# A graph network of four layers on one core: a third of every other attention unit's masking goes from VectorE to GpSimd

## The chip, the core and the metric

The kernel runs on one core of a Trainium2 chip. The core has five engines that run their own instruction streams and wait for one another by semaphores: TensorE (PE in the profile; its weight loads are listed apart as PEld), VectorE (DVE), ScalarE (ACT), GpSimd (POOL) and SyncE (SP), which here only issues DMAs. The metric is the device time of one execution in microseconds (us); lower is better.

## The reference

The input is x with 3327 nodes of 512 features, and a sparse adjacency matrix adj of 3327 x 3327, whose density falls with the node numbers. Four layers follow one another, each as x = x + layer(relu(layernorm(x)), adj). Layers 0, 2 and 3 are graph attentions with 8 heads of 64 features; layer 1 (SAGE) takes the mean of the neighbours and three products with 512 x 512 matrices. An attention, in short:

```python
Wh = h @ W                                  # per head: n x 64
e = leaky_relu(s_dst[i] + s_src[j])         # per head, for each pair (i, j)
e = where(adj[i, j] > 0, e, NEG)
out[i] = softmax_j(e) @ Wh                  # per head
```

Layer 0 then normalises its columns over the nodes and applies a relu; layers 2 and 3 apply an elu.

## The kernel before, in words

The nodes are padded to 26 blocks of 128. The work on a target side is done in 52 groups of 64 targets. Since adj is sparse, each group has a list of the sources that it needs, in chunks of 128 sources; the number of chunks is fixed per group (the table CAPS, from 22 for the first group to 5 and 4 for the last), 359 chunks in all. The lists are made in the first part of the kernel.

The softmax is taken apart so that no exponential is needed for a pair: exp(leaky_relu(a + b)) is the larger of two products of one factor of the target and one of the source. With a common factor taken out, one max per pair and head is left: the weight of source j for target i is max(r[i], v[j]) times the mask. The row sum comes from a 65th column of the features.

The function attend does one attention. A unit is 2 or 3 chunks of one group, 135 units per layer (89 of 3 chunks, 46 of 2). Per unit:

- load (L1240) gathers the source rows. The helper gather (L1164, L1165) issues one indirect DMA on the GpSimd queue per chunk: 128 rows of a table in DRAM, named by the list idx. A row holds the features and the factors v of all heads. The tile rows has 6 buffers. In layer 0 a row also holds the words of the adjacency; there load unpacks them on DVE (on, L1252) and ACT (mask, L1258) into the SBUF tile mask, which layers 1, 2 and 3 read again.
- DVE takes the max (mx, L1266) of r_bc, the group's target factors spread over all partitions in PSUM by a small matmul (L1198), and of the source factors in rows. The tile mx lies in PSUM and has one buffer.
- DVE multiplies mx with the mask (wgt, L1273) into SBUF, 3 buffers. The free size is 8 heads x 64 targets = 512 elements per chunk, so 1536 or 1024 per instruction.
- PE accumulates (facc, L1287): per chunk and head, wgt is the stationary operand and 65 columns of rows the moving one; the profile shows 16 matmul records per chunk.
- When a group ends, ACT copies the sums (L1215), DVE takes reciprocals (L1219), ACT scales (L1225), and for every second group finish adds the residual and stores.

The function later advances these endings by one step per unit, and with them, in layer 2, the projection of the next layer's features (tick), and in layer 0 small independent matmuls (beside).

Inside attend the order of instructions on PE, DVE and ACT is that of the program (manual_schedule). Pool is not in that list, so the planner orders its instructions; in attend Pool has nothing but the gathers. In the program load(i + 1) stands behind unit i's mult, and how far Pool runs ahead of the other engines is limited only by the 6 row buffers.

Of the kernel before, what the change touches and what calls it, by code (L numbers as in the profile page):

```python
# [23 lines left out]
F32 = mybir.dt.float32  # L24
# [3 lines left out]
I32 = mybir.dt.int32  # L28
# [4 lines left out]
ALU = mybir.AluOpType  # L33
ET = mybir.EngineType
# [4 lines left out]
P = 128  # L39
H = 8  # L40
F = 64
# [9 lines left out]
GB = 64  # L51
# [4 lines left out]
LNB = 5  # L56
ROW = H * (F + 1) + H
UNIT = 3
SUNIT = 2
SROWS = 8  # L60
SAHEAD = 2
# [1075 lines left out]
def sparse(ctx: ExitStack, tc: tile.TileContext, t: dict, out: bass.AP, WA, ls, cs, idx, rdeg, first):  # L1137
# [5 lines left out]
    nc = tc.nc  # L1143
# [18 lines left out]
    mask = keep.tile([P, NCH, GB], U8, name="mask")  # L1162

    def gather(dst, src, k):  # L1164
        nc.gpsimd.indirect_dma_start(  # L1165
            out=dst, out_offset=None, in_=src[:, :], in_offset=bass.IndirectOffsetOnAxis(ap=idx[:, k : k + 1], axis=0)
        )


    def attend(layer, table, r_dram, finish, tick=lambda: None, home=None):  # L1170

        width = table.shape[1]
        units = []
        for g in range(ls.G):
            mine = list(ls.batches(g, UNIT))
            units += [(g, k0, n, i == 0, i == len(mine) - 1) for i, (k0, n) in enumerate(mine)]
        hq = H // PG  # L1180
        sw = hq * (F + 1)
        with tc.tile_pool(name=f"fatt{layer}", bufs=2) as ap, tc.tile_pool(
            name=f"facc_ps{layer}", bufs=2, space=PSUM
        ) as aps, tc.manual_schedule(engines={ET.PE, ET.DVE, ET.Activation}):
            rows, rrs, rbs, accs, ends = {}, {}, {}, {}, []

            def fetch(g):
                if g < ls.G:
                    rr = ap.tile([2, H * GB], F32, name="r_two", tag="r_two", bufs=3)
                    nc.sync.dma_start(rr, r_dram[g, :, :, :].rearrange("t h i -> t (h i)"))  # L1190
                    rrs[g] = rr

            def spread(g):


                if g < ls.G:
                    rb = aps.tile([P, H * GB], F32, name="r_bc", tag="r_bc", bufs=2)
                    nc.tensor.matmul(rb, ones[0:2, :].bitcast(F32R), rrs.pop(g).bitcast(F32R), start=True, stop=True)  # L1198
                    rbs[g] = rb.rearrange("p (h i) -> p h i", i=GB)

            def ending(g, hps={}):

                b, u = divmod(g, PG)
                if u == 0:
                    hps[b] = home[:, b, :] if home is not None else None
                    if home is None:
                        hp_ = ap.tile([P, D], F32, name="fhp", tag="hp", bufs=3)
                        hps[b] = hp_
                hp, o0 = hps[b], u * GB
                fin = finish(b, hp, ap)  # L1210
                if u == PG - 1:
                    next(fin)
                yield
                sm = ap.tile([P, sw], F32, name="sums", tag="sums", bufs=4)
                nc.scalar.copy(sm, accs.pop(g)[:, :sw])  # L1215
                sm = sm.rearrange("p (q x) -> p q x", x=F + 1)
                yield
                rd = ap.tile([P, hq, 1], F32, name="rd", tag="rd", bufs=4)
                nc.vector.reciprocal(rd, sm[:, :, F : F + 1])  # L1219
                yield  # L1220
                for v in range(PG):
                    mine = slice(v * GB, (v + 1) * GB)
                    for q in range(hq):
                        h = q * PG + v
                        nc.scalar.mul(hp[o0 : o0 + GB, h * F : (h + 1) * F], sm[mine, q, 0:F], rd[mine, q, :])  # L1225
                yield
                if u == PG - 1:
                    del hps[b]
                    yield from fin

            def later():
                for e in list(ends):
                    if next(e, 0) == 0:
                        ends.remove(e)
                tick()

            for g in range(2):
                fetch(g)
            spread(0)
            def load(i):  # L1240

                if i >= len(units):
                    return
                g, k0, n, _, _ = units[i]
                gi = ap.tile([P, UNIT, width], I32, name="rows", tag="rows", bufs=6)
                rows[i] = gi.bitcast(F32)
                for k in range(n):
                    gather(gi[:, k, :], table, k0 + k)
                if layer == 0:
                    nw = GB // WB  # L1250
                    on = ap.tile([P, UNIT, nw, WB], U16, name="on", tag="on")
                    nc.vector.tensor_tensor(  # L1252
                        on[:, :n],
                        gi[:, :n, ROW:].bitcast(U16)[:, :, g * nw : (g + 1) * nw].unsqueeze(3).to_broadcast([P, n, nw, WB]),
                        cs["bit"].unsqueeze(1).unsqueeze(1).to_broadcast([P, n, nw, WB]),
                        ALU.bitwise_and,
                    )
                    nc.scalar.activation(mask[:, k0 : k0 + n, :], on[:, :n].rearrange("p k w b -> p k (w b)"), AF.Sign)  # L1258

            load(0)  # L1260
            for i, (g, k0, n, begins, stops) in enumerate(units):
                gt = rows.pop(i)
                mk = mask[:, k0 : k0 + n, :]
                full = [P, n, H, GB]
                mx = aps.tile([P, UNIT, H, GB], F32, name="mx", tag="mx", bufs=1)
                nc.vector.tensor_tensor(  # L1266
                    mx[:, :n],
                    rbs[g].unsqueeze(1).to_broadcast(full),
                    gt[:, :n, H * (F + 1) : ROW].unsqueeze(3).to_broadcast(full),
                    ALU.max,  # L1270
                )
                wt = ap.tile([P, UNIT, H, GB], F32, name="wgt", tag="wgt", bufs=3)
                nc.vector.tensor_tensor(wt[:, :n], mx[:, :n], mk.unsqueeze(2).to_broadcast(full), ALU.mult)  # L1273
                load(i + 1)
                later()
                if begins:
                    fetch(g + 2)
                    acc = aps.tile([P, BANK], F32, name="facc", tag="acc")
                    accs[g] = acc
                    spread(g + 1)  # L1280

                for k in range(n):
                    f, l = begins and k == 0, stops and k == n - 1
                    for q in range(hq):
                        for v in range(PG):
                            h = q * PG + v
                            nc.tensor.matmul(  # L1287
                                accs[g][v * GB : (v + 1) * GB, q * (F + 1) : (q + 1) * (F + 1)],
                                wt[:, k, h, :],
                                gt[:, k, h * (F + 1) : (h + 1) * (F + 1)],  # L1290
                                start=(f and q == 0),
                                stop=(l and q == hq - 1),
                            )
                if stops:
                    ends.append(ending(g))
            while ends:
                later()
# [32 lines left out]
    with ExitStack() as mx:  # L1330
# [48 lines left out]
        with tc.tile_pool(name="beside", bufs=1) as wp, tc.tile_pool(name="beside_ps", bufs=1, space=PSUM) as wps:  # L1379
            bg = beside(wp, wps)  # L1380

            def done(c, hp, pool):
                yield
                whole.append(c)
                yield

            attend(0, *first, done, lambda: next(bg, None), y)
            for _ in bg:
                pass
# [91 lines left out]
        def tick():  # L1481
            for e in list(ends):
                if next(e, 0) == 0:
                    ends.remove(e)
            proj.tick()
# [3 lines left out]
        for b in range(NB):  # L1489
            ps = list(zip_longest(*(list(ls.batches(b * PG + u, SUNIT)) for u in range(PG))))  # L1490
            parts += [(b, p, i == 0, i == len(ps) - 1) for i, p in enumerate(ps)]
        loaded = {}

        def load(i):
# [3 lines left out]
            for u, kn in enumerate(parts[i][1]):  # L1498
                if kn is not None:
                    k0, n = kn  # L1500
                    zt = gp.tile([P, SUNIT, D], F32, name="z_rows", tag="z_rows", bufs=SROWS)
                    mf = gp.tile([P, SUNIT, GB], F32, name="z_mask", tag="z_mask", bufs=SROWS)
                    nc.scalar.copy(mf[:, :n, :], mask[:, k0 : k0 + n, :])  # L1503
# [7 lines left out]
        for i, (b, _, begins, stops) in enumerate(parts):  # L1511
# [4 lines left out]
            for r, u, k, m, z in loaded.pop(i):  # L1516
# [3 lines left out]
                g = b * PG + u  # L1520
# [102 lines left out]
```

## Time and profile before

| | |
|---|---|
| median of 3 runs | 2915.1 us (2900.37 to 2917.88) |
| profiled execution | 2553.76 us, its span 2551.8 us |
| mean granted TensorE clock in it | 0.851 of full speed |
| mx L1266, wgt L1273 (DVE) | 405 instructions each, 639.4 and 638.4 us |
| rows L1165 (Pool gathers of the attentions) | 1077 instructions, 1027.7 us |
| facc L1287 (PE) | 17232 matmuls, 722.5 us |

One execution was profiled. Busy time is the time in which an engine runs an instruction; the idle time in front of a group of instructions is put down to what ended it. "issue" means that the engine waited for nothing that the profile shows. In the order of time: lists and the projection of layer 0 until 319 us, attention 0 until about 806 us, column statistics and layer 1 until about 1430 us, attention 2 until about 2010 us with layer 3's projection beside it, attention 3 from 2046 us to the end.

### The profile page before, as it was taken

To read this page: it belongs to the slowest core of one execution; us is meant where nothing else is said; L and a number is where in the kernel's file an instruction comes from. 1 tells how busy PE (TensorE), PEld (TensorE's weight loads), DVE (VectorE), ACT (ScalarE), POOL (GpSimd) and SP (SyncE) were. 2 spreads that over 40 slices of the span, in tenths; PEclk is the share of its full clock that TensorE was granted. 3 is DMA by queue.
4 is the path that set the end of the run, shared out by engine and by line. 5 is a ranking of instruction groups with operands and counts; after the bars stand their busy time and mean duration, and the time that the engine had idled before them with its cause. 6 is when DMAs were issued, how large, how long until landed. Compare 5 with 4: busy or idle time off the path is not lost.

```text
span 2551.8 us, 53690 instructions
## 1 busy us (share of the span) xinstructions
PE 1825.0 (72%) x21112; PEld 1161.8 (46%) x21112; DVE 1852.3 (73%) x2272; ACT 1068.3 (42%) x3810; POOL 1387.4 (54%) x1482
## 2 busy tenths in 40 slices
PE   3667756776677698889999657778878646566653
PEld 2444444454454342223333356656555435555543
DVE  7667579999997850222333499999877279999996
ACT  4553212333445332334455214667766601233444
POOL 1000176777772026777777277776554067777672
PEclk9767889988888899999999778897877787777787
DMA  8773198888783566788888478887665178888784
GB/s 326 288 263 123 43 296 276 280 281 260 241 253 95 191 217 198 234 247 260 254 267 255 125 223 242 235 240 232 199 200 177 39 215 232 236 238 243 232 238 123
DMA packets 189057, 562.57 MB, mean 220 GB/s; under 512 B 37764, under 2 KB 42304, under 8 KB 185470
## 3 DMA queue, kind: packets, MB, share of 16 engines
q0 software_dynamic: 115456, 404.86, 53.3%
q1 hardware_dynamic: 73342, 154.20, 17.0%
q8 instruction: 169, 2.77, 0.4%
q14 instruction: 90, 0.74, 0.1%
HBM read 499.26 MB, written 59.68 MB: 219 GB/s over the span
## 4 chain that ended last, share of the span: by engine, by line
PE 30%; DVE 24%; issue 13%; ACT 9%; DMA 8%; POOL 3%; DVEq 0%; SPq 0%; POOLq 0%; ACTq 0%
DVE mx L1266 12%; PE facc L1287 8%; DVE wgt L1273 8%; PE sage_acc L1522 4%; DMA z_rows<-h_dram,idx 4%; PE p_wh L866 4%; DMA rows<-table,idx 3%; PE n_ps L1471 3%; PE p_wh L808 3%; ACT fhp L1225 2%; POOL z_rows L1165 2%; PE s_ps L1445 2%; POOL rows L1165 1%; ACT bn_y L1225 1%; ACT v_row L870 1%
## 5 line engine op out<-in xcount | busy, mean ns | idle before, releaser
L1165 POOL DMA_INDIRECT rows<-table,idx x1077 | 1027.7, 954 | 580.0 <-issue 224.5
L1287 PE MATMUL facc<-rows,wgt 128*64 128x65 f32 x17232 | 722.5, 253 | 393.7 <-DVE wgt L1273 259.7
L1287 PEld LDWEIGHTS facc<-rows,wgt 128*64 128x64 f32 x17232 | 667.1, 165 | 518.2 <-DVE wgt L1273 310.5
L1266 DVE TENSOR_TENSOR mx<-r_bc,rows 128x1536 f32<-128x1536 f32 (+1 forms) x405 | 639.4, 1579 | 48.4 <-DMA fin_x<-fx 17.7
L1273 DVE TENSOR_TENSOR wgt<-mx,mask 128x1536 f32<-128x1536 f32 (+1 forms) x405 | 638.4, 1576 | 42.3 <-DVE mx L1266 1.0
L1165 POOL DMA_INDIRECT z_rows<-h_dram,idx x359 | 340.7, 949 | 273.7 <-ACT hT L1442 141.0
L1225 ACT ACTIVATE fhp<-sums,rd 64x64 f32<-64x64 f32 x832 | 219.9, 334 | 305.4 <-DVE rd L1219 302.0
L1522 PE MATMUL sage_acc<-z_rows,z_mask 128*64 128x512 f32 x718 | 209.8, 618 | 33.0 <-DMA z_rows<-h_dram,idx 32.6
L1258 ACT ACTIVATE mask<-on 128x192 uint8<-128x192 uint16 (+1 forms) x135 | 46.5, 345 | 325.3 <-DVE on L1252 321.8
L1086 POOL DMA_DIRECT2D list_b<-shift x12 | 6.0, 503 | 271.7 <-DVE shift L1040 271.5
L811 DVE TENSOR_TENSOR sd_pr<-p_wh,ab 128x1024 f32<-128x1024 f32 x26 | 31.8, 1225 | 141.4 <-PE p_wh L808 141.4
L1522 PEld LDWEIGHTS sage_acc<-z_rows,z_mask 128*64 128x64 f32 x718 | 52.2, 137 | 156.2 <-issue 77.6
L680 PE MATMUL wh_ps<-fWt,hT 128*128 128x512 f32 x208 | 123.3, 748 | 0.0
L866 PE MATMUL p_wh<-fWt,hT 128*128 128x512 f32 x208 | 117.2, 714 | 1.4 <-ACT s_col L860 1.4
L1225 ACT ACTIVATE bn_y<-sums,rd 64x64 f32<-64x64 f32 x416 | 109.5, 333 | 2.4 <-DVE rd L1219 0.5
L1503 ACT CAST z_mask<-mask 128x128 f32<-128x128 uint8 (+1 forms) x196 | 52.7, 284 | 118.7 <-PE sage_acc L1522 117.5
L1476 DVE TENSOR_TENSOR s_o<-n_ps,bn_y 128x512 f32<-128x512 f32 x26 | 17.9, 690 | 116.2 <-PE n_ps L1471 116.2
L1215 ACT COPY sums<-facc 128x260 f32<-128x260 f32 x156 | 56.6, 363 | 104.7 <-DMA rows<-table,idx 77.7
L1471 PE MATMUL n_ps<-fWx,aT 128*128 128x512 f32 x208 | 98.7, 608 | 0.0
L808 PE MATMUL p_wh<-fWt,hT 128*128 128x512 f32 x208 | 96.9, 610 | 2.0 <-DVE hT L699 1.9
L1445 PE MATMUL s_ps<-fWx,hT 128*128 128x512 f32 x208 | 93.5, 603 | 3.4 <-ACT hT L1442 3.4
L1198 PE MATMUL r_bc<-r_two,fones 2*128 2x512 f32 x156 | 89.1, 575 | 6.6 <-DMA r_two<-r_dram 3.6
(213 smaller groups left out, 2146.3 us busy)
## 6 DMA issues: line engine op xcount, KB each, us to landing
adj_i<-in_adj SPq DMA_DIRECT2D x26, 1664.0 KB
table<-v_row SPq DMA_DIRECT2D x78, 264.0 KB
rows<-table,idx POOLq DMA_INDIRECT x1077
fin_x<-fx SPq DMA_DIRECT2D x52, 256.0 KB
ln_x<-in_x SPq DMA_DIRECT2D x26, 256.0 KB
bn_x<-in_x SPq DMA_DIRECT2D x13, 512.0 KB
fx<-bn_x SPq DMA_DIRECT2D x13, 512.0 KB
fsage_x<-fx SPq DMA_DIRECT2D x26, 256.0 KB
```

Of the source, the lines that this page charges most:

```text
L680: nc.tensor.matmul(wh, hT[:, kc, :], self.Wt[:, kc, :], start=(kc == 0), stop=(kc == KC - 1))
L808: nc.tensor.matmul(wh, hT[:, kc, :], self.Wt[:, kc, :], start=(kc == 0), stop=(kc == KC - 1))
L866: nc.tensor.matmul(wh, hT[:, kc, :], self.Wt[:, kc, :], start=(kc == 0), stop=(kc == KC - 1))
L1165: nc.gpsimd.indirect_dma_start(out=dst, out_offset=None, in_=src[:, :], in_offset=bass.IndirectOffsetOnAxis(ap=idx[:, k : k + 1], axis=0))
L1198: nc.tensor.matmul(rb, ones[0:2, :].bitcast(F32R), rrs.pop(g).bitcast(F32R), start=True, stop=True)
L1225: nc.scalar.mul(hp[o0 : o0 + GB, h * F : (h + 1) * F], sm[mine, q, 0:F], rd[mine, q, :])
L1266: nc.vector.tensor_tensor(mx[:, :n], rbs[g].unsqueeze(1).to_broadcast(full), gt[:, :n, H * (F + 1) : ROW].unsqueeze(3).to_broadcast(full), ...
L1273: nc.vector.tensor_tensor(wt[:, :n], mx[:, :n], mk.unsqueeze(2).to_broadcast(full), ALU.mult)
L1287: nc.tensor.matmul(accs[g][v * GB : (v + 1) * GB, q * (F + 1) : (q + 1) * (F + 1)], wt[:, k, h, :], gt[:, k, h * (F + 1) : (h + 1) * (F + 1)],
L1445: nc.tensor.matmul(ps, hT[:, kc, :], Wx[:, 0, kc, :], start=(kc == 0), stop=(kc == KC - 1))
L1471: nc.tensor.matmul(ps, aT[:, kc, :], Wx[:, 1, kc, :], start=(kc == 0), stop=(kc == KC - 1))
L1522: nc.tensor.matmul(acc[u * GB : (u + 1) * GB, :], m, z, start=f, stop=l)
```

## The change

- In every unit with an odd index the last chunk is taken out of the unit's max and mult. DVE does its max by an instruction of its own, from r_bc and rows straight into wgt in SBUF, and Pool multiplies it there by the mask. The unit's remaining one or two chunks go through mx and wgt on DVE as before. Units with an even index are as before.
- The mask is bytes; for Pool's multiplication ACT copies the chunk's 64 columns to a float tile (mask_f, 3 buffers), one unit ahead (widened).
- Pool joins the list of engines whose order is that of the program. The gathers of unit i + 3 (AHEAD = 3) now stand ahead of unit i's max and multiplication, those of units 0 to 2 ahead of the loop.
- The unpacking of the adjacency in layer 0 is taken out of load into edges, which is called for unit i + 1 where load(i + 1) stood.

```diff
--- before.py
+++ after.py
@@ -56,6 +56,7 @@
 LNB = 5
 ROW = H * (F + 1) + H
 UNIT = 3
+AHEAD = 3
 SUNIT = 2
 SROWS = 8
 SAHEAD = 2
@@ -1181,7 +1182,7 @@
         sw = hq * (F + 1)
         with tc.tile_pool(name=f"fatt{layer}", bufs=2) as ap, tc.tile_pool(
             name=f"facc_ps{layer}", bufs=2, space=PSUM
-        ) as aps, tc.manual_schedule(engines={ET.PE, ET.DVE, ET.Activation}):
+        ) as aps, tc.manual_schedule(engines={ET.PE, ET.DVE, ET.Activation, ET.Pool}):
             rows, rrs, rbs, accs, ends = {}, {}, {}, {}, []
 
             def fetch(g):
@@ -1246,7 +1247,12 @@
                 rows[i] = gi.bitcast(F32)
                 for k in range(n):
                     gather(gi[:, k, :], table, k0 + k)
-                if layer == 0:
+
+            def edges(i):
+
+                if layer == 0 and i < len(units):
+                    g, k0, n, _, _ = units[i]
+                    gi = rows[i].bitcast(I32)
                     nw = GB // WB
                     on = ap.tile([P, UNIT, nw, WB], U16, name="on", tag="on")
                     nc.vector.tensor_tensor(
@@ -1257,10 +1263,32 @@
                     )
                     nc.scalar.activation(mask[:, k0 : k0 + n, :], on[:, :n].rearrange("p k w b -> p k (w b)"), AF.Sign)
 
-            load(0)
+            mps = {}
+
+            def widened(i):
+
+                if i < len(units) and i % 2:
+                    _, k0, n, _, _ = units[i]
+                    mp = mps[i] = ap.tile([P, GB], F32, name="mask_f", tag="mask_f", bufs=3)
+                    nc.scalar.copy(mp, mask[:, k0 + n - 1, :])
+
+            for i in range(AHEAD):
+                load(i)
+            edges(0)
             for i, (g, k0, n, begins, stops) in enumerate(units):
+                load(i + AHEAD)
                 gt = rows.pop(i)
                 mk = mask[:, k0 : k0 + n, :]
+                wt = ap.tile([P, UNIT, H, GB], F32, name="wgt", tag="wgt", bufs=3)
+
+                if i % 2:
+                    n -= 1
+                    one = [P, H, GB]
+                    nc.vector.tensor_tensor(
+                        wt[:, n], rbs[g], gt[:, n, H * (F + 1) : ROW].unsqueeze(2).to_broadcast(one), ALU.max
+                    )
+                    nc.gpsimd.tensor_tensor(wt[:, n], wt[:, n], mps.pop(i).unsqueeze(1).to_broadcast(one), ALU.mult)
+                    mk = mk[:, :n, :]
                 full = [P, n, H, GB]
                 mx = aps.tile([P, UNIT, H, GB], F32, name="mx", tag="mx", bufs=1)
                 nc.vector.tensor_tensor(
@@ -1269,16 +1297,17 @@
                     gt[:, :n, H * (F + 1) : ROW].unsqueeze(3).to_broadcast(full),
                     ALU.max,
                 )
-                wt = ap.tile([P, UNIT, H, GB], F32, name="wgt", tag="wgt", bufs=3)
                 nc.vector.tensor_tensor(wt[:, :n], mx[:, :n], mk.unsqueeze(2).to_broadcast(full), ALU.mult)
-                load(i + 1)
+                edges(i + 1)
                 later()
+                widened(i + 1)
                 if begins:
                     fetch(g + 2)
                     acc = aps.tile([P, BANK], F32, name="facc", tag="acc")
                     accs[g] = acc
                     spread(g + 1)
 
+                n = units[i][2]
                 for k in range(n):
                     f, l = begins and k == 0, stops and k == n - 1
                     for q in range(hq):
```

## The prediction

> **What bounds the kernel now.** I read the page's engine row first, then the costliest groups, then the three attentions one by one, and last the gather queue instruction by instruction.
>
> ```profile
> PE 1825.0 (72%) x21112; PEld 1161.8 (46%) x21112; DVE 1852.3 (73%) x2272; ACT 1068.3 (42%) x3810; POOL 1387.4 (54%) x1482
> ...
> L1165 POOL DMA_INDIRECT rows<-table,idx x1077 | 1027.7, 954 | 580.0 <-issue 224.5
> ...
> L1476 DVE TENSOR_TENSOR s_o<-n_ps,bn_y 128x512 f32<-128x512 f32 x26 | 17.9, 690 | 116.2 <-PE n_ps L1471 116.2
> ```
>
> By shares Pool is the engine with room, at 54%. But Pool has no work in long stretches, so the share says little about the stage that the change touches. The windows of the stages do; each runs from the first to the last gather of a part of an attention (columns: window, its length, busy time and instructions of each engine, clock, DMA). The lines are layer 0, layer 2 up to 1800 us, the rest of layer 2, and layer 3:
>
> ```profile
> 319.40:789.20 469.80, 316.42 (x5755) 230.52 (x5756) 441.15 (x445) 161.34 (x566) 341.28 (x359) 0.88 0.85 268
> 1447.70:1800.00 352.30, 257.11 (x4289) 202.77 (x4289) 328.25 (x306) 174.28 (x670) 251.79 (x264) 0.82 0.80 232
> 1800.00:1979.20 179.20, 145.71 (x1809) 105.59 (x1810) 136.85 (x166) 126.13 (x496) 90.84 (x95) 0.78 0.62 189
> 2046.50:2514.60 468.10, 274.75 (x5580) 242.14 (x5582) 443.84 (x355) 142.96 (x472) 343.75 (x359) 0.78 0.81 236
> ```
>
> DVE (third pair) is busy 94%, 93%, 76% and 95%, Pool (fifth) 73%, 71%, 51% and 73%. That still looks like a DVE bound with Pool room. The timeline of Pool shows that it isn't (start, length, and in brackets the idle time before it):
>
> ```profile
> 2185.17 0.95 POOL L1165 DMA_INDIRECT rows<-table,idx  x1 [0.30 <-issue]
> 2186.42 0.95 POOL L1165 DMA_INDIRECT rows<-table,idx  x1 [0.30 <-issue]
> 2187.67 0.94 POOL L1165 DMA_INDIRECT rows<-table,idx  x1 [0.30 <-issue]
> 2188.92 0.95 POOL L1165 DMA_INDIRECT rows<-table,idx  x1 [0.30 <-PE facc L1287]
> ```
>
> A gather occupies 0.95 us and there is never less than 0.30 us before the next, whatever is named as releaser: one slot is 1.25 us. A layer has 359 gathers, so Pool needs 359 x 1.25 = 449 us of the 470 us in layer 0 and of the 468 us in layer 3 (96%). In layer 2 it needs 264 x 1.25 = 330 us of the first 352 us (94%), and 95 x 1.25 = 119 us of the last 179 us, where PE is busy 81% and sets the pace with the projection of the next layer. So the attentions of layers 0 and 3, and two thirds of layer 2, stand on DVE and Pool alike, with only about 20 us of slack on Pool in each.
>
> **What the Trainium skill says.** (1) "GPSIMD Engine Reference", section 3.1: a Pool tensor_tensor add of 2048 fp32 elements takes 4497 ns, because its two inputs share one read port. The trace before has no two-input Pool operation; its one-output fill of 384 elements takes 408 ns and of 1664 elements 1484 ns, which is 0.84 us per thousand elements and some 0.09 us fixed. (2) "VectorE: DVE Perf Modes", section on the TRN2 errata: a fp32 tensor_tensor takes (N+151)/0.96 ns, so 1757, 1224 and 691 ns for 1536, 1024 and 512 elements. The trace agrees: 1761 (mx) and 1758 (wgt), 1227 and 1225, and 690 (the s_o row above, one input in PSUM, output in SBUF). (3) "SBUF — State Buffer", section "Who interferes with whom": a DVE operation with at most one SBUF input does not contend with Pool. All the max and mult operations have one input in PSUM (r_bc, or mx), so I count no lock; no run here shows it yet.
>
> **The change, part by part.** There are 135 units in a layer, 89 of 3 chunks and 46 of 2; 67 have an odd index.
>
> *DVE in an odd unit.* With 3 chunks it had 1761 + 1758 = 3519 ns; now 690 for the last chunk's max into SBUF, 1227 + 1225 for the other two chunks: 3142 ns. With 2 chunks 1227 + 1225 = 2452 becomes 3 x 690 = 2070. It saves 0.38 us, times 67 = 25 us in a layer, 76 us in three. That is worth time only while DVE ends last.
>
> *Pool in an odd unit.* One multiplication of 128x512. From the skill's figure, 4497 x 512/2048 = 1.12 us; with 0.09 us fixed from the fills, 1.2 us (estimates). What gap goes with it isn't shown: before a gather there is 0.30 us anyway, between fills there is none. I take 1.25 us as its whole slot. Lower end 0.9 us (part of the work fits into the 0.30 us gap), upper end 2.0 us (a gap of its own, a slower loop for the broadcast mask, waits for DVE). Some 65 of the 67 lie between the first and last gather: 65 x 1.25 = 81 us per layer.
>
> *Layer 0:* Pool then needs 449 + 81 = 530 us, with 5 us left over for waits 535 us, against 470: **+65 us**. DVE falls to about 441 - 25 = 416 us and waits. *Layer 3:* 535 against 468: **+67 us**. *Layer 2:* first part 330 + 47 x 1.25 + 5 = 394 against 352: **+42 us**; the rest needs 119 + 20 x 1.25 = 144 of 179 us and stays PE's: 0.
>
> *Order on Pool.* Three units' gathers stand ahead of each multiplication, and behind it the next three chunks. The multiplication waits for the max of its own unit, whose rows were gathered some 12 us earlier (three units of 4 us); the chain before shows 3.4 to 3.7 us for rows to land, so the max is long done and Pool doesn't stand: 0. If DVE were late, the gathers behind would stand too, and the price would be that lateness. The lead itself gives nothing: before, Pool issued without a stop from 319 us on until the six row buffers were full, thus it was further ahead than three units. Range 0 to -5 us per layer.
>
> *PE* gets the last chunk of an odd unit from Pool instead of DVE. With Pool the bound, PE follows it; this is in the sums. Its row buffers come free later, but the gather that needs one is three units behind: 0.
>
> *ScalarE* widens a 128x64 mask in 67 units, about 0.28 us each (the 128x128 mask casts of layer 1 take 292 ns): 19 us per layer beside 143 to 300 us busy. Hidden under Pool; in layer 2's PE-paced end, where PE and ScalarE alternate, at most 20 x 0.28 = 6 us. Nothing is added to SP's queue; the edge words of layer 0 are unpacked by DVE in the same place as before.
>
> **The sum.** Against the profiled execution (span 2551.8, time 2553.8 us) it is 65 + 42 + 67 = +174 us. The runs shown have a median of 2915.1 us, 361 us above it, and no view says where those lie. The profile's granted TensorE clock varies between stages (0.76 to 0.97), and the stages outside the attentions with long runs of matmuls (the SAGE layer from 1021 us, PE busy 83%) stretch with it; so I take a lower clock in these runs as the cause. Then PE covers part of the new Pool time: layer 2's first part had PE busy 257 of 352 us at clock 0.82, which at 0.55 would fill the stage: I count 10 of the 42. Layer 0 (316 of 470 at 0.88) would come near the bound by itself: I count 50 of the 65. Layer 3 (275 of 468 at 0.78) keeps its 67. Together +127, thus about **3040 us**, 4.3% slower.
>
> **Rivals.**
> - *PE hides most of it.* In the runs shown layers 0 and 2 are already paced by PE, and only layer 3 and a little of layer 0 pay: +35 to +70, around 2975 us. For it: 361 us unexplained. Against it: PE's 316 us in layer 0 would have to grow by half.
> - *Pool's multiplication costs far more* (2.0 us or a lock against DVE): layer 0 and 3 need 449 + 130 + 5 = 584 us, +115 each, layer 2 some +20: about 3165 us. For it: no two-input Pool row exists before. Against: the port rule above and the fills.
> - *Faster: DVE ends last after all.* The place is layers 0 and 3: if the multiplication slips into the 0.30 us gaps, its slot tends to nothing and DVE's 25 us per layer show, but not past Pool's own 449 us: at most 20 us in each of layers 0 and 3 and some 20 in layer 2, 2855 us. It decides where 449 + 65 m + 5 is below 469, so at m below 0.23 us per multiplication; even one pass over 512 elements at the fill's rate is 0.43 us. At m = 0.23 nothing changes.
> - The change doesn't do what it says: the order written by hand leaves Pool's gathers as they were and the multiplication stands, so I see no such case, only that of a different clock in the runs after.
>
> **Chances.** Forecast (2990 to 3095) 0.60; PE hides most 0.17 (a third of it within 1%); costlier multiplication 0.12; faster or another clock regime 0.07; no change 0.04. The range leaves out the faster case and the far end of the costly one: 2965 to 3125. What a measurement can tell from no change is about 1%: faster 0.07, same 0.08, slower 0.85.
>
> **What would show it.** Right: Pool's row of gathers unchanged at 0.95 us, a new Pool group of 201 multiplications of some 1.2 us, Pool filling its stretches without idle time, the windows of layers 0 and 3 near 535 us, DVE busy below 80% there and waiting, and PE's waits turning from DVE wgt to the Pool line. Wrong: multiplications that overlap the gaps (slots below 0.5 us), Pool standing behind DVE's max with gathers queued behind, DVE operations longer than before (a lock), or stages outside the attentions that move, which would be the clock and not the change.

## The result, and the profile after

The kernel after takes 2928.61 us (median of 9 runs, 2911.33 to 2943.26), the kernel before 2911.84 us (9 runs, 2900.37 to 2918.11): a ratio of 1.0066, interval 1.0042 to 1.0089. The forecast was 3040 us, 4.3% slower, with a range from 2965 us. The change makes the kernel slower, as forecast, but by 17 us instead of 127.

The page of the kernel after, a profiled execution of 2943.26 us (engine row, then costliest groups: name and count, busy us and mean ns, idle time before and what ended most of it):

```profile
PE 2135.0 (73%) x21112; PEld 1355.0 (46%) x21112; DVE 1839.6 (63%) x2473; ACT 1107.5 (38%) x4011; POOL 1653.4 (56%) x1683
...
L1166 POOL DMA_INDIRECT rows<-table,idx x1077 | 1037.5, 963 | 537.4 <-issue 228.7
L1316 PE MATMUL facc<-rows,wgt 128*64 128x65 f32 x17232 | 994.3, 269 | 455.0 <-issue 417.9
...
L1290 POOL TENSOR_TENSOR wgt<-wgt,mask_f 128x512 f32<-128x512 f32 x201 | 256.1, 1274 | 102.2 <-ACT mask_f L1273 93.2
L1287 DVE TENSOR_TENSOR wgt<-r_bc,rows 128x512 f32<-128x512 f32 x201 | 138.3, 688 | 213.8 <-PE facc L1316 150.6
```

The parts of the change are there at about their estimated prices: 201 Pool multiplications of 1.27 us (1.2 estimated), 201 DVE max operations of 0.69 us (0.69). What wasn't foreseen is in PE's row: PE sits idle for 418 us before its own matmuls, and the profile names no releaser, only issue. In the profile before that was 98 us (what waited, what ended the wait, us in total, times, the longest):

```profile
PE facc L1287 <- DVE wgt L1273: 259.7, 177, 14.3
POOL rows L1165 <- PE facc L1287: 149.9, 165, 5.0
PE facc L1287 <- issue: 97.6, 47, 3.4
```

And even these 98 us were no idle time without a reason: each of the 47 waits ends within 0.15 us after a DVE instruction finished a piece of wgt, so PE got its weights there, and issue stands only for a releaser that the profile missed. By the same count 373 of the 418 us of the kernel after do not end so. Waits of this second kind are called pauses from here on; the profile before has none. Here are the three attentions of the same execution from first to last gather (window, length, busy time and instructions of PE, PEld, DVE, ACT and POOL, clock, DMA):

```profile
326.40:898.30 571.90, 408.53 (x5746) 291.39 (x5746) 471.63 (x511) 178.69 (x638) 424.98 (x423) 0.78 0.73 220
1639.10:2279.90 640.80, 486.82 (x6070) 355.49 (x6072) 450.58 (x536) 308.71 (x1224) 428.60 (x424) 0.76 0.64 180
2347.10:2909.40 562.30, 389.09 (x5611) 316.98 (x5611) 421.80 (x424) 161.34 (x544) 429.49 (x424) 0.68 0.69 196
```

Each attention takes 94 to 109 us longer than in the profile before (470, 531 and 468 us). But the nine runs of the two kernels differ by 17 us. So the profile before and the runs before can't have shown the same behaviour, and the first question was what the kernel before does in an execution of 2912 us.

The kernel before takes 2909 to 2953 us on some chips and 2555 to 2556 us on others, and each group of experiments below fell on one chip, so its results are compared with the runs of the kernel before on that same chip.

### The profile page after: what moved, and what is told of

Same layout as the page of the kernel before. It is cut to its first block, busy times and chain, and to the rows that moved or that the text cites. A ratio compares the mean times of both kernels' runs of the same rounds, so it can differ in the third digit from the quotient of the medians.

```text
span 2941.4 us, 54744 instructions
## 1 busy us (share of the span) xinstructions
PE 2135.0 (73%) x21112; PEld 1355.0 (46%) x21112; DVE 1839.6 (63%) x2473; ACT 1107.5 (38%) x4011; POOL 1653.4 (56%) x1683
## 4 chain that ended last, share of the span: by engine, by line
PE 42%; issue 13%; ACT 6%; DVE 4%; another core or an unknown queue 2%; DMA 1%; POOL 1%; SPq 0%; DVEq 0%; ACTq 0%; POOLq 0%
PE facc L1316 20%; PE p_wh L867 4%; PE sage_acc L1551 4%; PE p_wh L809 3%; PE n_ps L1500 3%; PE r_bc L1199 2%; PE p_sd L854 1%; PE s_ps L1474 1%; ACT fhp L1226 1%; POOL z_rows L1166 1%; ACT v_row L871 1%; PE p_ps L801 1%; ACT hT L849 1%; PE p_ps L846 1%
## 5 line engine op out<-in xcount | busy, mean ns | idle before, releaser
L1316 PE MATMUL facc<-rows,wgt 128*64 128x65 f32 x17232 | 994.3, 269 | 455.0 <-issue 417.9
L1316 PEld LDWEIGHTS facc<-rows,wgt 128*64 128x64 f32 x17232 | 841.1, 177 | 674.6 <-issue 598.2
L1300 DVE TENSOR_TENSOR wgt<-mx,mask 128x1024 f32<-128x1024 f32 (+2 forms) x405 | 531.3, 1312 | 92.1 <-PE facc L1316 49.7
L1294 DVE TENSOR_TENSOR mx<-r_bc,rows 128x1024 f32<-128x1024 f32 (+2 forms) x405 | 530.4, 1310 | 31.3 <-DMA rows<-table,idx 29.6
L1290 POOL TENSOR_TENSOR wgt<-wgt,mask_f 128x512 f32<-128x512 f32 x201 | 256.1, 1274 | 102.2 <-ACT mask_f L1273 93.2
L1287 DVE TENSOR_TENSOR wgt<-r_bc,rows 128x512 f32<-128x512 f32 x201 | 138.3, 688 | 213.8 <-PE facc L1316 150.6
L1551 PE MATMUL sage_acc<-z_rows,z_mask 128*64 128x512 f32 x718 | 200.9, 625 | 8.9 <-DMA z_rows<-h_dram,idx 7.9
L867 PE MATMUL p_wh<-fWt,hT 128*128 128x512 f32 x208 | 127.7, 768 | 1.8 <-ACT s_col L861 1.4
L809 PE MATMUL p_wh<-fWt,hT 128*128 128x512 f32 x208 | 109.3, 674 | 18.7 <-ACT hT L804 12.8
L1258 DVE TENSOR_TENSOR on<-rows,fbit 128x192 uint16<-128x192 uint16 (+1 forms) x135 | 100.8, 746 | 12.4 <-DMA rows<-table,idx 12.0
```

What stands on the lines that cost most here:

```text
L809: nc.tensor.matmul(wh, hT[:, kc, :], self.Wt[:, kc, :], start=(kc == 0), stop=(kc == KC - 1))
L867: nc.tensor.matmul(wh, hT[:, kc, :], self.Wt[:, kc, :], start=(kc == 0), stop=(kc == KC - 1))
L1258: nc.vector.tensor_tensor(on[:, :n], gi[:, :n, ROW:].bitcast(U16)[:, :, g * nw : (g + 1) * nw].unsqueeze(3).to_broadcast([P, n, nw, WB]), ...
L1287: nc.vector.tensor_tensor(wt[:, n], rbs[g], gt[:, n, H * (F + 1) : ROW].unsqueeze(2).to_broadcast(one), ALU.max)
L1290: nc.gpsimd.tensor_tensor(wt[:, n], wt[:, n], mps.pop(i).unsqueeze(1).to_broadcast(one), ALU.mult)
L1294: nc.vector.tensor_tensor(mx[:, :n], rbs[g].unsqueeze(1).to_broadcast(full), gt[:, :n, H * (F + 1) : ROW].unsqueeze(3).to_broadcast(full), ...
```

## The experiments

**The kernel before and the kernel after, unchanged, on one chip (e1, e2).** No edit.

> The kernel before, unchanged, to get a profile of an execution at the time of its runs (about 2912 us). Theory A (PE's own instruction stream paces the attentions in these executions): facc shows 350 us or more of idle time put down to issue, as the kernel after does (418 us), where the profile on record shows 98 us; the attentions take about 100 us more each than in that profile. Theory B (the change made PE stall; the kernel before is slow for another reason): facc's issue idle stays near 100 us, and the 360 us lie outside the attentions or in longer matmuls at a lower clock.

> The kernel after, unchanged, beside the kernel before on one chip. Both theories: 2915 to 2945 us, +0.5 to +1%. Its profile is for a comparison with the profile of e1 stage by stage: by theory A each attention is within 15 us of that of e1; by theory B the attentions are some 60 us longer each and something outside is shorter.

The kernel before took 2953.0 us; e1, the same kernel, 2946.6 us, ratio 0.9963 (0.9930 to 0.9996), which shows how far two sets of runs of one kernel lie apart on such a chip; e2 took 2982.9 us, 1.0096 (1.0067 to 1.0125). The page of e1:

```profile
PE 2114.3 (72%) x21112; PEld 1338.9 (45%) x21112; DVE 1856.7 (63%) x2272; ACT 1071.4 (36%) x3810; POOL 1391.5 (47%) x1482
...
L1165 POOL DMA_INDIRECT rows<-table,idx x1077 | 1030.3, 957 | 877.1 <-PE facc L1287 386.0
L1287 PE MATMUL facc<-rows,wgt 128*64 128x65 f32 x17232 | 975.5, 267 | 434.7 <-issue 397.3
```

and its attentions, then those of e2:

```profile
318.40:890.70 572.30, 406.95 (x5748) 286.46 (x5746) 445.16 (x445) 165.19 (x570) 340.50 (x359) 0.80 0.71 220
1647.70:2276.40 628.70, 463.40 (x6072) 345.41 (x6074) 465.74 (x470) 299.30 (x1162) 342.95 (x359) 0.77 0.63 183
2342.20:2910.10 567.90, 393.47 (x5622) 320.06 (x5622) 448.28 (x357) 149.57 (x481) 344.06 (x359) 0.67 0.67 194
```

```profile
320.40:898.50 578.10, 425.86 (x5747) 303.25 (x5747) 464.87 (x511) 179.12 (x637) 424.64 (x423) 0.74 0.71 218
1657.50:2304.10 646.60, 473.58 (x6076) 349.84 (x6077) 450.83 (x536) 308.99 (x1225) 428.84 (x424) 0.77 0.61 179
2372.10:2946.80 574.70, 393.26 (x5620) 323.78 (x5621) 419.68 (x423) 160.84 (x544) 430.22 (x423) 0.66 0.66 192
```

Theory A holds, theory B falls: the kernel before has the idle time of PE as well (397 us, 370 of them pauses), and its attentions take 572, 629 and 568 us here. Only layer 2 of e2, 18 us longer than in e1, is a little outside the 15 us that theory A allowed. In layer 0 the 358 steps from first to last gather need 358 x 1.25 = 448 us, so Pool stands for 125 us there, 181 us in layer 2 and 120 us in layer 3, mostly until PE gives back a row buffer (386 us in the row above, 150 us in the profile before). In the timeline of e1 PE gets stuck within a unit whose weights are complete:

```profile
2404.09 0.34 PE L1287 MATMUL facc<-rows,wgt 128*64 128x65 f32 x4 [0.43 <-issue]
...
2404.81 0.37 PE L1287 MATMUL facc<-rows,wgt 128*64 128x65 f32 x5 [0.39 <-issue]
...
2405.57 0.38 PE L1287 MATMUL facc<-rows,wgt 128*64 128x65 f32 x5 [0.39 <-issue]
...
2407.04 1.58 PE L1287 MATMUL facc<-rows,wgt 128*64 128x65 f32 x34 [1.09 <-issue]
```

Four or five matmuls in 0.35 us, 0.4 us of nothing, again and again, and then 34 at once in 1.58 us. No other engine is named. A lower clock isn't it either: layer 3 has 0.67 here, and e9 further down has 0.68 there without a pause. The three attentions hold 300 of the 392 us by which this execution is longer than the one profiled before, and layer 1 with the column statistics (757 against 659 us) holds the rest. In layers 0 and 3 PE's busy time and pauses together make 547 of 572 and 548 of 568 us, so PE paces them.

**Half of PE's instructions (e3, e4).** In both kernels the same edit; the two heads of a pair share one matmul, with the first head's features.

```diff
-                        for v in range(PG):
-                            h = q * PG + v
-                            nc.tensor.matmul(
-                                accs[g][v * GB : (v + 1) * GB, q * (F + 1) : (q + 1) * (F + 1)],
-                                wt[:, k, h, :],
...
+                        h = q * PG
+                        nc.tensor.matmul(
+                            accs[g][:, q * (F + 1) : (q + 1) * (F + 1)],
+                            wt[:, k, h : h + PG, :].rearrange("p h i -> p (h i)"),
...
```

> The kernel before with half of the attentions' matmuls left out: the two heads of a pair share one matmul, with the features of the first (so the second head's output is wrong). Theory A: with half of PE's stream gone, DVE and Pool pace the attentions, and the time falls by 250 us or more, to some 2500 to 2650 us. Theory B: DVE and Pool paced them already, and it falls by less than 80 us.

> The kernel after with the same half of the matmuls left out. Theory A: Pool is now the bound, since it has 1.25 us per gather and 1.27 us per multiplication: the attentions of layers 0 and 3 take about 535 us where those of e3 take 470, and the whole is 100 to 190 us slower than e3. Theory B: within 30 us of e3.

Both expectations failed, because the edit does the opposite of what it was made for: e3 takes 3172.8 us (ratio 1.0757, 1.0696 to 1.0817) and e4 3161.9 us (1.0704, 1.0674 to 1.0734). The row of e3:

```profile
L1286 PE MATMUL facc<-rows,wgt 128*128 128x65 f32 x8616 | 1619.5, 374 | 54.5 <-issue 41.7
```

Half as many matmuls are busy for 1620 us instead of 975. In e1 6757 of the 17232 matmuls start within 0.03 us of the one before, in e3 none starts within 0.05 us; it looks as if the tiles 64 columns wide run beside each other in pairs and those 128 wide don't. The granted clock was lower as well (0.70 against 0.79). PE is heavier than before, busy 87% of the span. That makes it a test from the other side: with PE the bound beyond doubt, the change costs nothing (3161.9 against 3172.8 us), and Pool's 257 us of multiplications vanish altogether.

**Zero weights, and only the last chunk (e5 to e8).** e5 and e6: the mask is written as zeros, with 1e-5 added to the row sums. e7 and e8: PE accumulates only the last chunk of each unit, with the same addition. e5 and e7 are made from the kernel before, e6 and e8 from the kernel after.

```diff
-                nc.scalar.copy(sm, accs.pop(g)[:, :sw])
+                nc.scalar.activation(sm, accs.pop(g)[:, :sw], AF.Identity, bias=eps_t)
...
-AF.Sign)
+AF.Sign, scale=0.0)
```

```diff
-                for k in range(n):
-                    f, l = begins and k == 0, stops and k == n - 1
+                for k in range(n - 1, n):
+                    f, l = begins, stops
```

> The kernel before with the mask written as zeros (so the weights of all attentions and of the SAGE layer are zero and the outputs wrong; 1e-5 is added to the row sums so that their reciprocals stay finite). Every engine runs the same instructions on the same addresses. Theory A1 (the idle time inside facc that no record explains, 397 us in e1, is a brake on PE's power, which depends on what its array switches): the idle time goes and the time falls to 2550 to 2700 us. Theory A2 (it comes from how instructions or semaphores reach PE): within 2% of the kernel before.

> The kernel after with the same zero mask. Theory A1: PE out of the way, the attentions of layers 0 and 3 stand on Pool at 535 us where e5 has 470, and the whole is 100 to 190 us slower than e5. Theory A2: within 1.5% of e5.

> The kernel before with only the last chunk of each unit accumulated by PE (the others' matmuls are left out, outputs wrong, 1e-5 added to the row sums): 2160 instead of 5744 matmuls in a layer, of the same form. PE is out of the way by both theories; DVE and Pool pace the attentions: about 470 us from first to last gather in each, 2550 to 2680 us in all.

> The kernel after with only the last chunk of each unit accumulated. If Pool's slots add (1.25 us per gather, 1.27 us per multiplication) the three attentions take about 535 us each and the whole is 130 to 200 us slower than e7. If the multiplication fits into the gaps of the gathers, it is within 40 us of e7 or faster.

These fell on a chip where the kernel before itself takes 2555.6 us, so e5, at 2556.5 us (1.0005, 0.9997 to 1.0014), says nothing between A1 and A2. Two other things follow. e7, with 62% of the attentions' matmuls gone, takes 2556.5 us (1.0001, 0.9994 to 1.0008): on such a chip PE is no bound in the attentions. And there the change costs what the sum said in kind: e6 2700.4 us (1.0569, 1.0551 to 1.0586), e8 2696.0 us (1.0552, 1.0534 to 1.0570), some 140 us above e5 and e7.

**The change unchanged and in parts (e9 to e12).** e10 keeps the order written by hand, the gathers three units ahead and edges, but splits no unit. e11 splits as the change does, but DVE multiplies.

```diff
-                if i % 2:
+                if False:
...
-                if i < len(units) and i % 2:
+                if False:
```

```diff
-                    nc.gpsimd.tensor_tensor(wt[:, n], wt[:, n], mps.pop(i).unsqueeze(1).to_broadcast(one), ALU.mult)
+                    nc.vector.tensor_tensor(wt[:, n], wt[:, n], mps.pop(i).unsqueeze(1).to_broadcast(one), ALU.mult)
```

> The kernel after, unchanged. Where the kernel before takes about 2555 us (as beside e5 to e8): the Pool bound shows, +5% to +6.5% (2690 to 2720 us), the attentions of layers 0 and 3 at about 530 us. Where the kernel before takes about 2912 to 2955 us: +0.5 to +1.2% again.

> The order alone: Pool by hand, gathers three units ahead, the unpacking moved to edges, but no unit is split and Pool multiplies nothing. I expect no difference from the kernel before on either kind of chip (within 0.5%): Pool has nothing but gathers, and it ran ahead before. Rival: the lead held to three units costs when a unit's PE work is irregular, +0.5 to +1% where the kernel before takes 2912 to 2955 us, and is then all of the loss there.

> The kernel after, but DVE multiplies the split chunk too (in SBUF, by the float mask): Pool has the gathers alone, DVE some 0.69 - 0.38 = 0.31 us more per odd unit than before, 21 us per layer. Where the kernel before takes 2555 us: DVE ends last in layers 0 and 3, +1% to +2.5%, less than half of the loss of e9. Where it takes 2912 us or more: PE paces, within 0.7% of the kernel before.

> The kernel before with the zero mask of e5 again. On a chip where the kernel before takes 2912 us or more it tells A1 from A2: by A1 (PE's pauses depend on what its array switches) the time falls by at least 5%, by A2 it stays within 2%. On a chip where the kernel before takes 2555 us: equal within 0.3%, as in e5.

Again a chip with 2556.1 us for the kernel before. The kernel after takes 2698.2 us, ratio 1.0565 (1.0542 to 1.0589), 142 us more. Its page:

```profile
L1166 POOL DMA_INDIRECT rows<-table,idx x1077 | 1039.2, 965 | 424.4 <-issue 234.8
L1316 PE MATMUL facc<-rows,wgt 128*64 128x65 f32 x17232 | 801.5, 267 | 481.6 <-POOL wgt L1290 400.5
```

PE's waits have turned to Pool's line, 400 us of them. The attentions of e9, and Pool's queue around one multiplication:

```profile
320.70:846.80 526.10, 349.00 (x5779) 254.86 (x5778) 460.14 (x515) 179.03 (x642) 424.71 (x423) 0.82 0.77 239
1501.10:2064.30 563.20, 414.45 (x6070) 316.78 (x6072) 460.18 (x536) 308.12 (x1224) 430.23 (x424) 0.79 0.70 205
2133.50:2664.30 530.80, 324.80 (x5673) 288.37 (x5675) 431.42 (x426) 160.65 (x548) 430.08 (x423) 0.68 0.71 208
```

```profile
2233.30 0.94 POOL L1166 DMA_INDIRECT rows<-table,idx  x1 [0.30 <-issue]
2234.26 1.27 POOL L1290 TENSOR_TENSOR wgt<-wgt,mask_f 128x512 f32<-128x512 f32 x1
2235.70 0.98 POOL L1166 DMA_INDIRECT rows<-table,idx  x1 [0.16 <-issue]
2236.98 0.95 POOL L1166 DMA_INDIRECT rows<-table,idx  x1 [0.31 <-issue]
```

From gather to gather it is 2.40 us with a multiplication between and 1.25 us without: a slot of 1.15 us (2.40 is also the median of 195 such distances in this trace, 1.25 that of 879 without), since the multiplication starts 0.02 us after the gather and the next gather follows after 0.16 us instead of 0.30. 448 + 65 x 1.15 = 523 us; layers 0 and 3 took 526 and 531 us. Pool is full.

e10 takes 2555.1 us (0.9998, 0.9990 to 1.0005): the order and the lead cost and give nothing, as expected. e11 takes 2692.1 us (1.0537, 1.0519 to 1.0555), where +1 to +2.5% was expected. Its row:

```profile
L1290 DVE TENSOR_TENSOR wgt<-wgt,mask_f 128x512 f32<-128x512 f32 x201 | 139.5, 694 | 163.0 <-ACT mask_f L1273 146.2
```

The multiplication takes its 0.69 us, but DVE stands 146 us for the float mask (94 in layer 0, 52 in layer 2), whose copy can lie in ScalarE's queue behind the 8 scalings of a group's ending (8 of 0.33 us). So e11 didn't measure what it was made for. e12 equals the kernel before, as e5.

**The rest of the open points (e13 to e18).** e13 repeats e5; e14 and e17 repeat e7; e15 and e18 repeat e8. e16 is e11 with the byte mask and without the copy:

```diff
-                    nc.gpsimd.tensor_tensor(wt[:, n], wt[:, n], mps.pop(i).unsqueeze(1).to_broadcast(one), ALU.mult)
+                    nc.vector.tensor_tensor(wt[:, n], wt[:, n], mask[:, k0 + n, :].unsqueeze(1).to_broadcast(one), ALU.mult)
...
-                if i < len(units) and i % 2:
+                if False:
```

> The kernel before with the zero mask of e5 again, for a chip on which the kernel before takes 2912 us or more. A1 (PE's pauses depend on what its array switches): at least 5% faster than the kernel before. A2 (they don't): within 2%. On a chip where the kernel before takes 2555 us: within 0.3%.

> The kernel before with only the last chunk of each unit accumulated by PE, as e7. Where the kernel before takes 2912 us or more, theory A (PE paces the attentions there) says that it falls by 200 to 350 us, with the attentions near 470 us from first to last gather, as e7 has on the other chip. Where it takes 2555 us: as e7.

> The kernel after with only the last chunk of each unit accumulated, as e8. Theory A, on either kind of chip: with PE out of the way Pool is the bound, so layers 0 and 3 take 525 to 535 us and the whole is 110 to 160 us slower than e14. If something other than PE hid Pool's multiplications where the kernel before takes 2912 us, it is within 50 us of e14 there.

> As e11, but DVE multiplies the split chunk by the byte mask itself, so there is no float mask and no copy on ScalarE. If e11 was slow because DVE stood behind these copies (146 us of waits), this one loses only DVE's 0.31 us per odd unit, 21 us per layer: +1% to +2.5% where the kernel before takes 2555 us. If the cost was the split itself, it stays at +4% or more. Where the kernel before takes 2912 us or more: within 1%.

> As e14, for a chip on which the kernel before takes 2912 us or more: by theory A the attentions fall to about 470 us from first to last gather and the whole by 200 to 350 us. Elsewhere as e7.

> As e15, for a chip on which the kernel before takes 2912 us or more: by theory A 110 to 160 us slower than e17; if something other than PE hid Pool's multiplications there, within 50 us of e17. Elsewhere as e8.

e13 to e16 met a chip with 2555.4 us once more. e13 (1.0002, 0.9991 to 1.0013) leaves A1 and A2 undecided for good: the zero mask never ran where the pauses are. e14 (0.9998) and e15 (1.0547, 1.0526 to 1.0568) repeat e7 and e8. e16 takes 2582.2 us, 1.0108 (1.0084 to 1.0133), with 12 us of idle time left before its multiplication: the split itself costs 27 us, DVE's longer work, and the rest of e11 goes with the copies.

e17 and e18 met a chip with pauses (the kernel before 2909.1 us). e17 takes 2786.0 us (0.9545, 0.9479 to 0.9612) and e18 2796.8 us (0.9605, 0.9536 to 0.9674): 11 us apart, where theory A said 110 to 160. Layers 0 and 3 of e17, then of e18:

```profile
323.90:845.90 522.00, 305.03 (x2257) 170.00 (x2256) 441.38 (x443) 168.16 (x565) 339.65 (x359) 0.58 0.76 240
...
2240.00:2761.10 521.10, 210.77 (x2148) 154.69 (x2148) 447.37 (x357) 152.80 (x481) 341.79 (x359) 0.50 0.71 211
```

```profile
322.50:851.30 528.80, 270.32 (x2275) 151.94 (x2274) 454.87 (x515) 182.62 (x642) 425.63 (x424) 0.58 0.76 237
...
2230.70:2761.70 531.00, 171.25 (x2148) 134.51 (x2148) 432.29 (x426) 163.01 (x546) 429.16 (x424) 0.50 0.71 207
```

e18 is where Pool's sum puts it, at 529 and 531 us, the same as on the other kind of chip (526 and 531 in e9). What failed is the assumption on e17: with 38% of the matmuls left, PE is still not out of the way, and the attentions take 522 us where e7 has 467. The same edit that changed nothing on the quick chip (1.0001) makes the kernel 4.5% faster here, so PE's matmuls do pace the attentions here, but something remains. PE's rows of e7 and then of e17, and a piece of e17's timeline (remote stands for a releaser that the profile can't name):

```profile
L1287 PE MATMUL facc<-rows,wgt 128*64 128x65 f32 x6480 | 413.4, 299 | 557.7 <-DVE wgt L1273 394.0
L1287 PE MATMUL facc<-rows,wgt 128*64 128x65 f32 x6480 | 478.8, 300 | 618.9 <-issue 451.5
```

```profile
2601.26 0.27 PE L1287 MATMUL facc<-rows,wgt 128*64 128x65 f32 x1 [1.37 <-issue]
2602.65 0.81 PE L1287 MATMUL facc<-rows,wgt 128*64 128x65 f32 x10 [1.13 <-issue]
2602.80 1.76 DVE L1273 TENSOR_TENSOR wgt<-mx,mask 128x1536 f32<-128x1536 f32 x1 [1.77 <-remote]
...
2607.59 1.76 DVE L1273 TENSOR_TENSOR wgt<-mx,mask 128x1536 f32<-128x1536 f32 x1
2609.45 1.14 PE L1287 MATMUL facc<-rows,wgt 128*64 128x65 f32 x16 [2.98 <-issue]
```

The 451 us under issue are not all pauses. The last two lines show a wait of 2.98 us that ends 0.10 us after DVE has finished the weights; 312 of the 451 us end in this way. The first two lines are pauses, and there DVE stands too (1.77 us) and goes on 0.15 us after PE. 139 us of pauses are left, 38% of e1's 370, as the matmuls are 38%. They don't fill the stage, for PE's busy time and pauses make only 368 of 522 us in layer 0, but with only a few buffers between the engines they can hold up DVE: DVE's idle time before its max and multiplications is 189 us in e17 and 83 us in e7. That these 139 us alone make the 55 us per attention is not shown.

The runs but e17 fit one rule: an attention of layer 0 or 3 lasts about as long as the longest of DVE (about 467 us before), Pool (448 us before, 523 to 531 us after) and PE with its pauses (none on one kind of chip; some 550 to 570 us on the other with all matmuls). In e17 no engine is busy throughout; there DVE's work and its waits for PE seem to add up.

## Why the prediction was wrong, point by point

**The step that failed** is the last of the sum: the 361 us between the profiled execution and the runs were taken for a lower clock, felt mainly *outside* the attentions, and PE was let hide only 47 of the 174 us. e1 shows most of them *inside*: its attentions take 102, 97 and 100 us more than those of the profile, 300 of 392 us, with pauses of PE that no view before showed. With 120 to 181 us of standing in each attention, Pool has room for 65 x 1.15 = 75 us, and only 6, 18 and 7 us of it come through (e1 against e2), 31 us, where the whole grew by 30 us (36 against e1's own runs). The term was 127 us and measured 17, or 30 in e2. The rival that PE hides most named the right mechanism, but still let layer 3 pay; the measured +0.66% falls into what the chances called the same, with 0.08.

**The sum against the profiled execution** was of the right kind. Where the kernel before takes about 2554 us, as in the profile, the change costs 142 us against the 174 of the sum (e9). Layer by layer: +56, +32 and +63 us, forecast +65, +42 and +67. That 142 lies near the 127 of the forecast is chance: 47 us had been taken off for a PE that hides nothing there. The clock at which PE would fill layer 2's first part was also worked out wrongly: 257 us at 0.82 become 352 us at 0.60, not 0.55. The slot was taken as 1.25 us and is 1.15; the multiplication was well estimated, the gap around it shrinks. That Pool and not DVE is the engine that counts, in spite of 54% busy, is shown by e9 (PE waits for POOL wgt 400 us) and by the pair e9 and e16 in layers 0 and 3; in layer 2 the late copies (below) are mixed in.

**DVE's gain** of 25 us per layer came to nothing, as said. One price was left out: the unpacking in layer 0 (on) has two SBUF inputs, and with Pool reading SBUF it grew from 44 us in the profile before to 87 us in e9:

```profile
L1252 DVE TENSOR_TENSOR on<-rows,fbit 128x192 uint16<-128x192 uint16 (+1 forms) x135 | 44.1, 326 | 11.7 <-DMA rows<-table,idx 11.7
L1258 DVE TENSOR_TENSOR on<-rows,fbit 128x192 uint16<-128x192 uint16 (+1 forms) x135 | 87.0, 644 | 50.7 <-DMA rows<-table,idx 50.3
```

In e9 the 53 that overlap a Pool multiplication take 1.14 us in the mean and the other 82 take 0.32 us; in e10, e11 and e16, where Pool multiplies nothing, all take 0.32 to 0.33 us in the mean. This agrees with what the Trainium skill says in "SBUF — State Buffer", section "Who interferes with whom": a DVE instruction with two SBUF inputs contends with a GpSimd instruction that reads SBUF. I had applied that only to max and mult, whose times (1.76 and 1.22 us) indeed didn't move. The prediction had named longer DVE operations as a sign of being wrong. Layer 0 of e9 lasts only 3 us more than Pool's sum, so this is hidden.

**The order on Pool**: e10 shows 0, as forecast. The 3.4 to 3.7 us read for the landing of rows are only some of the chain's pieces (most of them 3.1 to 5.2 us), but 12 us of lead cover these too. **ScalarE's copies** were put at 0 to 6 us; they were late, and Pool stood 93 us for them in the kernel after (47 us in e9). In e9 4 of the 47 us lie in layer 0, 44 in layer 2 and none in layer 3. So layers 0 and 3 leave at most a few us for them, but how much of layer 2's 32 us is theirs is open, since no run had the copies earlier on Pool's version.

**Open:** what makes PE pause on some chips. The number of matmuls alone doesn't set it: e17 and e18 have the same 6480 on one chip, with 139 us of pauses and 1.7. In e18 PE waits 680 us for Pool's pieces of wgt, and e3, where PE is busiest, has only 16.5 us of pauses, which speaks against the brake of theory A1 without deciding it; what the matmuls compute wasn't tried on such a chip. Each of the five chips of the experiments was used in one session, so the chip itself and its state at that time aren't told apart. The profile before shows no pauses; on which chip it was taken isn't known.

## What to carry to other kernels

When a profiled execution and the timed runs of the same kernel lie 14% apart, the profile doesn't show what bounds the runs: find where the difference lies before pricing a change, or give each place that it could lie in a case of its own. An engine's free share is not its slack: count its slot from start to start (here 1.25 us for a gather of 0.95) against the stage. And a cost moved onto a full engine may still show nothing, if a third engine is later yet; on a chip where that one is quicker, it shows in full. Nor does "issue" prove that an engine waited for nothing: see whether one of its inputs was finished just before.

## What the runs showed of the hardware that was not expected

- Chips differ: the same kernel takes 2555 to 2556 us on three of them and 2909 to 2953 us on two, with PE pausing for 0.4 us after every four or five matmuls in parts of a unit on the latter (370 us in e1; 139 in e17 with 38% of the matmuls; 1.7 in e18, where PE waits for Pool). The same change is worth 0.7 to 1.0% on one kind and 5.65% on the other.
- A Pool multiplication of 1.27 us between two gathers lengthens their distance by only 1.15 us.
- A stationary tile of 128 columns took PE 1620 us for 8616 matmuls, tiles of 64 columns 975 us for 17232 (e3 and e1, at clocks of 0.70 and 0.79).
- The DVE operation with two SBUF inputs lengthens beside Pool's multiplications: on goes from 0.32 us to 1.14 us in the mean where the two overlap (e9).
